# A two-layer vision tower: turning tokens for layer-1 attention with VectorE block transposes and DRAM transfers instead of TensorE transposes

## The chip, the core and the metric

The kernel runs on one core of one Trainium2 chip. Its engines are TensorE (PE in the profile; PEld is its weight load), VectorE (DVE), ScalarE (ACT), GpSimd (POOL) and SyncE (SP), which here only issues DMAs. The metric is the device time of one execution in microseconds, as the median of a few runs. All data are float32.

## The reference, cut to what matters

Thirty-two images of 256 tokens with 256 features pass a tokenizer, layer 0 (gated attention, then a feed-forward on selected tokens), and layer 1. The change is in the attention of layer 1 and, for two pairs of images, in the end of layer 0. Per image it computes:

```
x   = layernorm(h)                       # the kernel's norm; rows are tokens
k   = tanh(gelu(x @ Wk1 + bk1) @ Wk2 + bk2) * freq * pi
q   = tanh(gelu(x @ Wq1 + bq1) @ Wq2 + bq2) * freq * pi
V   = x @ Wv + bv
r_t = sum over s <= t, k-phases of cos(k_s - q_t) * V_s  / sqrt(64 (t+1))
h   = h + x + (layernorm(r) * ln_w + ln_b) @ Wo + bo
```

The products x @ Wk1 and x @ Wq1 contract over features. TensorE contracts over partitions, so it needs x with features on partitions (`dxT`), while the norm yields x with tokens on partitions (`dx`). Making `dxT` from `dx` is what is changed.

## The kernel before, in words

The whole tower stays on the chip. `H[b]` holds image b as [128 partitions, 2 chunks of 128 tokens, 256 features]. The stages run one after the other: tokenizer, attention of layer 0, feed-forward of layer 0 (`step_c`, images in groups of four), attention of layer 1 (functions with `_d`), feed-forward of layer 1. The order of every engine's instructions in these stages is written out by hand: an engine does its own in program order and waits on semaphores for the others. SP is an engine of this kind too, its DMAs stand in one queue in program order.

Layer-1 attention goes by pairs of images, 16 of them. The loop over t at line 988 starts one pair every three steps, and in each step calls the functions for whichever pairs they are due (`do(step, which)` calls `which` for pair u where t = 3u + step). For pair u these are, in the order of a pair's life:

- step 0: `norm_d` (L789), which makes the two images' `dx` from `H` on VectorE: per image two short operations for `one` (L796, L797) and two TENSOR_SCALARs of 128x256 (L799). `dx` has four buffers, one per image, so two pairs' worth.
- step 1: `turn` (L891). It calls `transposed` (L180), in which TensorE transposes 128x128 blocks, eight per pair (L189), into two PSUM banks; ScalarE (L194) and VectorE (L196) copy these to `dxT`, [128 features, 2 halves, 512 tokens]. Also `residual_d` (L805): GpSimd adds `dx` and a bias row to `H`, four additions of 128x512 (L808, L809).
- step 2: `hidden` (L895) twice, for keys and queries: matmuls on `dxT` and a Gelu.
- step 3: `phases` (L906): matmuls, tanh, then VectorE arithmetic (L923 to L927) and a sine on ScalarE.
- step 4: `match` (L930): scores of all token pairs on TensorE; VectorE multiplies them by a causal matrix into `dat` (L943).
- step 5: `memory` (L946): TensorE with `dx` as weights and `dat`; it is the last reader of the pair's `dx`.
- step 6: `output` (L959): matmuls with `wvo` into four banks, and statistics on VectorE (L967).
- step 7: `add_output` (L974) and `stats_e` (L979).

A steady round of TensorE, three steps, is so in program order: turn of pair u, match of u-1, hidden of u, memory of u-1, phases of u, output of u-1. In the step of hidden u and memory u-1 the buffers that pair u+1 will get for its `dx` are those that memory u-1 reads. Calls out of this order are made at the start: pairs 0 and 1 are normed at the end of layer 0's feed-forward (L873 to L875, into buffers `cx`), both are turned early (t = 1 and 2), and pair 1's steps are drawn ahead. At t = 6, 9 and 12 the last group of layer 0's `step_c` fetches and updates its four images (fetches on GpSimd, updates L849 and L124 on VectorE).

Within layer 0's feed-forward, buffers `cs` [128, 4, 256], two of them, receive a group's selected tokens (`first_ranks`, L220), and `made` (L823) stores its results to DRAM through SP (L830, `results`).

Of the kernel before, what the change touches and what calls it, by code (L numbers as in the profile page):

```python
# [33 lines left out]
F32 = mybir.dt.float32  # L34
# [6 lines left out]
P = 128  # L41
B, N, D = 32, 256, 256
NC = N // P
# [37 lines left out]
def vit_tower(tc, a, out):  # L81

    nc = tc.nc
# [13 lines left out]
    def bank():  # L97
        return ppool.tile([P, 512], F32, name="bank", tag="bank")
# [19 lines left out]
    def over(ap, shape, axis):  # L118
        return ap.unsqueeze(axis).to_broadcast(shape)
# [46 lines left out]
    def at(pair, b):  # L166

        st, rs = pair[b // HALF]
        return st, rs, b % HALF
# [10 lines left out]
    def transposed(xT, xs, copy):  # L180


        w = len(xs) * N
        for k in range(2):
            p = bank()
            for j, x in enumerate(xs):
                for c in range(NC):
                    o = j * N + c * P
                    nc.tensor.transpose(p[:, o : o + P], x[:, c, k * P : (k + 1) * P], ident)  # L189
            copy(k, xT[:, k, :], p[:, 0:w])  # L190
# [13 lines left out]
    pdram = passing_x.enter_context(tc.tile_pool(name="c_d", bufs=1, space=bass.MemoryType.DRAM))  # L204
# [8 lines left out]
    p0 = region_c0.enter_context(tc.tile_pool(name="c_0", bufs=1, reuse_waits="tile"))  # L213
# [59 lines left out]
    with (  # L273
# [7 lines left out]
        for k, n in enumerate(PARTS):  # L281
            f = sum(PARTS[:k])
            x, w = pw.tile([P, n, N], F32, name=f"patch0_{k}"), pw.tile([P, n, D], F32, name=f"tokW{k}")
# [4 lines left out]
        p = bank()  # L288
# [62 lines left out]
        for b in range(B):  # L351
# [12 lines left out]
            if b in (B - 6, B - 4):  # L364
                u = (b - B + 6) // 2
# [39 lines left out]
    with (  # L405
# [71 lines left out]
        def turn_weights(b0):  # L477
            p = bank()
            for j in range(2):
                w = normed_c[b0][j][1]  # L480
                for c in range(NC):
                    o = j * N + c * P
                    nc.tensor.transpose(p[:, o : o + P], w[:, c : c + 1].to_broadcast([P, P]), ident)  # L483
            return p
# [17 lines left out]
        for t in range(B // 2 + 2):  # L502
# [4 lines left out]
            if t >= 4:  # L507
                turned = turn_weights(2 * (t - 4))
# [108 lines left out]
    for i in range(2):  # L617
        s, t = slice(i * HD, (i + 1) * HD), slice((1 - i) * HD, (2 - i) * HD)
# [170 lines left out]
    def norm_d(b0, s, pool, name, bufs):  # L789
        s.xs = []  # L790
        for j in range(2):
            x = pool.tile([P, NC, D], F32, name=name, bufs=bufs)
            st, rs, i = at(st_d, b0 + j)
            q = slice(i * NC, (i + 1) * NC)
            one = spool.tile([P, NC], F32, name="d_one")
            nc.vector.scalar_tensor_tensor(one, st[:, i, :, 0], -1.0, rs[:, q], ALU.mult, ALU.mult)  # L796
            nc.vector.tensor_scalar(one, one, 1.0, None, ALU.add)  # L797
            for c in range(NC):
                nc.vector.tensor_scalar(  # L799
                    x[:, c, :], H[b0 + j][:, c, :], rs[:, i * NC + c : i * NC + c + 1], one[:, c : c + 1],  # L800
                    ALU.mult, ALU.add,
                )
            s.xs.append(x)

    def residual_d(b0, s):  # L805
        for j in range(2):
            h = H[b0 + j]
            nc.gpsimd.tensor_tensor(h, h, s.xs[j], ALU.add)  # L808
            nc.gpsimd.tensor_tensor(h, h, over(add_row, [P, NC, D], 1), ALU.add)  # L809

    with region_c:
        st_d = new_stats("d")

        def hidden_c(b0, s, half):
            if half == 0:
                s.hT = p2.tile([P, 8, 4 * P], F32, name="hT")
            for m in range(4 * half, 4 * half + 4):
                p = bank()
                for k in range(2):
                    mm(p, w1[:, k, m * P : (m + 1) * P], s.xsel[:, k, :], k == 0, k == 1)  # L820
                nc.scalar.activation(s.hT[:, m, :], p, AF.Gelu_apprx_tanh, bias=col("b1", m))

        def made(b0, s, half):  # L823
            for j in range(2 * half, 2 * half + 2):
                p = bank()
                for m in range(8):
                    mm(p[:, 0:D], s.hT[:, m, j * P : (j + 1) * P], w2[:, m, :], m == 0, m == 7)
                y = p2.tile([P, D], F32, name="cy", bufs=4)
                nc.vector.tensor_tensor(y, p[:, 0:D], row_c("b2"), ALU.add)
                nc.sync.dma_start(results[b0 + j][:], y)  # L830

        def fetch(b0, s, half):
            s.y = s.y if half else []
            for b in range(b0 + 2 * half, b0 + 2 * half + 2):
                y = px.tile([P, NC, D], F32, name="cx", bufs=8)
                for c in range(NC):
                    k = b * NC + c
                    nc.gpsimd.indirect_dma_start(
                        y[:, c, :], None, results[b][:], bass.IndirectOffsetOnAxis(rank_of[:, k : k + 1], 0)
                    )  # L840
                s.y.append(y)

        def update(b0, s, half):
            for j in range(2 * half, 2 * half + 2):
                b = b0 + j
                st, rs, i = at(st_d, b)
                for c in range(NC):
                    k = b * NC + c
                    nc.vector.scalar_tensor_tensor(  # L849
                        H[b][:, c, :], s.y[j][:, c, :], w_kept[:, k : k + 1], H[b][:, c, :], ALU.mult, ALU.add  # L850
                    )
                    stats(st, i, c, H[b][:, c, :])
            pow_rstd_of(st_d, b0 + 2 * half, 2)

        ORDER_C = ((0, hidden_c, 0), (1, hidden_c, 1), (2, made, 0), (-1, turn_c, 0), (-8, first_ranks, 0),
                   (3, made, 1), (4, fetch, 0), (5, fetch, 1), (5, update, 0), (6, update, 1))

        def step_c(t):  # L860
            for at_step, do, j in ORDER_C:
                u, r = divmod(t - at_step, 4)
                if r == 0 and 0 <= u < B // 4 and (u > 1 or do is not first_ranks):
                    do(4 * u, quads[u], j)

        END_C = 4 * (B // 4 - 1) + 4
        pairs = [Pair() for _ in range(B // 2)]
        preparing = prepare()
        for t in range(END_C):
            if t == 0:  # L870
                norms_c(B - 2)
                residuals_c(B - 2)
            if t == END_C - 2:  # L873
                for u in range(2):
                    norm_d(2 * u, pairs[u], px, "cx", 8)  # L875
            step_c(t)
            if t < 2:
                ranks(B - 4 + 2 * t, turn_weights(B - 4 + 2 * t))
            if t >= 8:
                next(preparing, None)  # L880
        passing.close()
# [5 lines left out]
    with (  # L887
        tc.tile_pool(name="d_2", bufs=2, reuse_waits="tile") as p2,
        tc.tile_pool(name="d_8", bufs=8, reuse_waits="tile") as p8,
    ):  # L890
        def turn(b0, s):  # L891
            s.xT = p2.tile([P, 2, 2 * N], F32, name="dxT")
            transposed(s.xT, s.xs, copy_split)

        def hidden(b0, s, i, ms=(0, 1)):  # L895

# [91 lines left out]
        for t in range(3 * (NP - 1) + 8):  # L988
            def do(step, which, *more):
                u, r = divmod(t - step, 3)  # L990
                if r == 0 and 0 <= u < NP:
                    which(2 * u, pairs[u], *more)

            last = t == 3 * NP + 1
            if t != 4:
                do(1, turn)
            if not last:
                do(7, add_output)
            if t != 4:
                do(4, match)  # L1000
            if last:
                output(B - 4, pairs[NP - 2], (3,))
                add_output(B - 4, pairs[NP - 2])
            do(7, stats_e)
            if t != 4:
                do(1, residual_d)
            do(2, hidden, 0)
            if t == 2:
                do(2, hidden, 1)
                turn(2, pairs[1])  # L1010
            elif t == 5:
                do(2, hidden, 1, (0,))
                match(0, pairs[0])
                do(2, hidden, 1, (1,))
            else:
                do(2, hidden, 1)
            do(5, memory)
            do(3, phases)
            if t == 5:
                residual_d(2, pairs[1])  # L1020
            if t > 3:
                do(0, norm_d, p8, "dx", 4)
            if t == 3 * NP:
                output(B - 4, pairs[NP - 2], (0, 1, 2))
            else:
                do(6, output)
            if t in (6, 9, 12):
                step_c(END_C + (t - 6) // 3)
# [5 lines left out]
    with (  # L1034
# [27 lines left out]
        def turned(b, im):  # L1062
            im.xT = p1.tile([P, 2, N], F32, name="exT")
            nc.scalar.copy(im.xT.rearrange("p k n -> p (k n)"), im.pt)
# [422 lines left out]
        p = bank()  # L1487
# [381 lines left out]
```

## Time and profile before

| | us |
|---|---|
| median of 3 runs (1919.85 to 1925.09) | 1921.87 |
| the profiled execution | 1921.73 |
| its span in the profile | 1919.9 |
| PE busy | 1876.7 (98%) |
| VectorE busy | 1255.8 (65%) |
| ScalarE busy | 814.9 (42%) |
| GpSimd busy | 757.3 (39%) |
| PE transposes of layer-1 attention (L189, `cx` of pairs 0 and 1, `dx` of the others) | 128 instructions, 0.27 each |

All places in time are microseconds from the start of the span. Layer-1 attention lies between about 929 and 1272 us. In this stage DMAs move 1 to 25 GB/s, against 306 in the kernel's first slice. A line of the timeline or of the chain has the start, the duration, then the engine, source line, and operation with its tiles; what stands in brackets at its end is the engine's idle time before it and what ended it. The chain of waits follows the end of the program back from what released what, so a stretch of it that is all PE is a stretch in which nothing but PE's own work sets the time. Matmuls of float32 are listed as two instructions each, transposes as one.

### The profile page before, as it was taken

What the parts mean: (1) busy time and instruction counts of PE and PEld (TensorE: products, weight loads), DVE (VectorE), ACT (ScalarE), POOL (GpSimd) and SP (SyncE); (2) the same over time, 40 slices, a digit from 0 to 9 for tenths busy, and PEclk for the clock granted to TensorE, in tenths of its full rate; (3) what the DMA queues carried; (4) which work ended last, traced back from release to release, by engine and by line L of the source; (5) the groups of instructions that cost most, each with busy time, mean ns of one, the idle gap of its engine ahead of it and who ended that gap; (6) DMA issues with size and microseconds to landing.
All of it is one profiled execution on the core that took longest, in us unless ns stands there. A gap on an engine that the chain in (4) does not pass through costs nothing.

```text
span 1919.9 us, 36937 instructions
## 1 busy us (share of the span) xinstructions
PE 1876.7 (98%) x14852; PEld 1337.1 (70%) x14852; DVE 1255.8 (65%) x3257; ACT 814.9 (42%) x1646; POOL 757.3 (39%) x792
## 2 busy tenths in 40 slices
PE   9999999999999999999999999999999999999993
PEld 8887666666666676766655555568878878787872
DVE  2334456565657573434366556544999999999988
ACT  0001322222222212122343444447787888878772
POOL 1224223333343344334253333334454545455453
PEclk9999999999999999999999999999999999999995
DMA  9450000000000132222000000001222222222212
GB/s 306 152 150 15 1 17 25 25 17 17 15 19 14 41 113 83 61 75 63 12 22 1 1 1 1 1 13 24 60 54 63 57 57 63 52 62 57 63 40 57
DMA packets 69506, 94.49 MB, mean 49 GB/s; under 512 B 8656, under 2 KB 51152, under 8 KB 68944
## 3 DMA queue, kind: packets, MB, share of 16 engines
q1 hardware_dynamic: 62608, 74.49, 13.6%
q0 software_dynamic: 6144, 16.79, 2.8%
q8 instruction: 119, 1.95, 0.4%
q10 hardware_dynamic: 576, 0.79, 0.1%
q14 instruction: 59, 0.48, 0.1%
HBM read 46.41 MB, written 20.97 MB: 35 GB/s over the span
## 4 chain that ended last, share of the span: by engine, by line
PE 95%; DVE 4%; issue 0%; DMA 0%; ACT 0%; POOL 0%; SPq 0%; DVEq 0%; ACTq 0%
PE bank L116 91%; PE bank L772 2%; PE bank L189 1%; DMA patch<-in_patches_dram 0%; PE bank L230 0%; PE bank L483 0%; DVE six L124 0%; DVE fout L1367 0%; DVE fout L1381 0%; DVE eo L1245 0%; DVE ranges L1268 0%; DVE six L967 0%; DVE fout L1370 0%; DVE h L849 0%; DVE ey L1330 0%
## 5 line engine op out<-in xcount | busy, mean ns | idle before, releaser
L1164 POOL TENSOR_SCALAR_AFFINE_SELECT et<-et 128x512 f32<-128x512 f32 (+1 forms) x192 | 165.7, 875 | 203.3 <-ACT et L1155 201.3
L1155 ACT ACTIVATE et<-bank 128x512 f32<-128x512 f32 x384 | 207.7, 630 | 30.6 <-PE bank L116 30.3
L116 PE MATMUL bank<-ev,et 128*64 128x68 f32 (+1 forms) x6144 | 200.6, 226 | 0.0
L116 PEld LDWEIGHTS bank<-ev,et 128*64 128x64 f32 x6144 | 193.1, 138 | 5.7 <-issue 4.7
L116 PE MATMUL bank<-g,sx 64*128 64x512 f32 (+1 forms) x512 | 177.6, 486 | 0.0
L116 PE MATMUL bank<-g,sw 64*128 64x512 f32 (+1 forms) x512 | 177.2, 486 | 0.0
L116 PE MATMUL bank<-tokW,patch 128*128 128x256 f32 x768 | 168.0, 382 | 1.7 <-DMA patch<-in_patches_dram 1.7
L116 PEld LDWEIGHTS bank<-tokW,patch 128*128 128x128 f32 x768 | 146.8, 191 | 23.2 <-issue 2.7
L116 PE MATMUL bank<-bxT,w_wuv 128*128 128x512 f32 x300 | 131.4, 592 | 0.0
L1184 ACT COPY eo<-bank 128x280 f32<-128x280 f32 x256 | 96.1, 395 | 70.1 <-PE bank L116 62.8
L116 PEld LDWEIGHTS bank<-g,sx 64*128 64x128 f32 x512 | 93.1, 187 | 31.8 <-issue 22.9
L116 PE MATMUL bank<-wvo,dm 128*128 128x512 f32 x256 | 114.3, 599 | 0.0
L116 PE MATMUL bank<-attn,bv 128*128 128x256 f32 x512 | 113.1, 379 | 0.0
L116 PE MATMUL bank<-w_wo,gT 128*128 128x256 f32 x512 | 113.1, 379 | 0.0
L116 PE MATMUL bank<-w_w,hT 128*128 128x256 f32 x512 | 113.1, 379 | 0.0
L116 PE MATMUL bank<-xsel,w_w 128*128 128x512 f32 x256 | 111.4, 592 | 0.0
L116 PEld LDWEIGHTS bank<-attn,bv 128*128 128x128 f32 x512 | 97.2, 190 | 19.6 <-issue 6.9
L124 DVE BATCH_NORM_STATS2 six<-h 128x6 f32<-128x256 f32 x256 | 105.5, 412 | 4.4
L116 PEld LDWEIGHTS bank<-w_w,hT 128*128 128x128 f32 x512 | 96.6, 190 | 15.3 <-issue 2.9
L116 PEld LDWEIGHTS bank<-g,sw 64*128 64x128 f32 x512 | 93.1, 187 | 20.1 <-issue 9.9
L116 PEld LDWEIGHTS bank<-w_wo,gT 128*128 128x128 f32 x512 | 97.2, 190 | 13.2
L116 PE MATMUL bank<-w_wuv,bxT 128*128 128x512 f32 x240 | 105.4, 592 | 0.0
(275 smaller groups left out, 3688.8 us busy)
## 6 DMA issues: line engine op xcount, KB each, us to landing
patch<-in_patches_dram SPq DMA_DIRECT2D x31, 768.0 KB, 4.8
sw<-sx SPq DMA_DIRECT2D x64, 128.0 KB, 2.4
out_dram<-fout SPq DMA_DIRECT2D x32, 256.0 KB, 2.7
both<-fxT SPq DMA_DIRECT2D x62, 128.0 KB, 2.3
both<-hx SPq DMA_DIRECT2D x62, 128.0 KB, 2.3
cs<-ranked SPq DMA_DIRECT2D x32, 128.0 KB, 3.0
results<-cy SPq DMA_DIRECT2D x32, 128.0 KB, 1.7
w_w<-in_w_dram SPq DMA_DIRECT2D x2, 1024.0 KB, 8.3
```

The source lines that it names most:

```text
L116: nc.tensor.matmul(o, lhsT, rhs, start=first, stop=last)
L124: nc.vector.bn_stats(six, x)
L189: nc.tensor.transpose(p[:, o : o + P], x[:, c, k * P : (k + 1) * P], ident)
L772: nc.tensor.transpose(p[:, o : o + P], x[:, c, k * P : (k + 1) * P], ident)
L1155: nc.scalar.activation(t2[:, i, :], p, AF.Exp)
L1164: nc.gpsimd.affine_select(out=own, in_=own, pattern=[[0, 2 * n_e], [1, P]], compare_op=ALU.is_ge, fill=0.0, base=0, channel_multiplier=-1,)
L1184: nc.scalar.copy(im.o[:, g * OC : (g + 1) * OC], p[:, 0:OC])
```

## The change

`turn`, with TensorE's transposes, is gone from this stage. In its place:

- `blocks_d`: for each image of a pair VectorE transposes 32x32 blocks of `dx` (one instruction per image, 128x512) into a buffer y; then SP issues four DMAs, one for each 32 partitions of y, that store it to a DRAM tile `d_turned`. Each stores 1024 pieces of 128 B, 512 B apart. The two image halves and the chunk order are so placed that a partition of `dxT` lies in two contiguous runs of 2 KB.
- `turned`: four DMAs on SP load `dxT`, 32 partitions each, in pieces of 2 KB (64 per DMA).
- `norm_d`, `blocks_d` and `turned` of pairs 2 to 15 are called at the end of step -1 instead of norm at the end of step 0 and turn at the start of step 1. That is behind hidden and memory of the pairs before, and ahead of the next phases on VectorE. The buffers y of these pairs are one (`dxB`).
- Pairs 0 and 1 have their blocks transposed and stored at the end of layer 0's feed-forward, right behind their norms, with the two `cs` buffers as y; they are loaded at t = 1 and t = 2 of the stage.

TensorE's remaining instructions, and those of ScalarE and GpSimd but for ScalarE's copies of `dxT`, keep their order.

```diff
+    def blocks_d(b0, s, pool, name, shape, bufs):
+        y = pool.tile(shape, F32, name=name, bufs=bufs).rearrange("p j (f t) -> p (j f t)", t=32)
+        y = y.rearrange("p (f c t) -> p f c t", f=8, t=32)
+        for j, x in enumerate(s.xs):
+            nc.vector.transpose(
+                y[:, :, j * NC : (j + 1) * NC, :].rearrange("p f c t -> p c f t"),
+                x.rearrange("p c (f t) -> p c f t", t=32),
+            )
+        s.d = pdram.tile([32, 16 * NC, 4, 32], F32, name="d_turned", bufs=2)
+        for i in range(4):
+            nc.sync.dma_start(s.d[:, :, i, :], y[32 * i : 32 * i + 32].rearrange("p f c t -> p (f c) t"))
+
...
             if t == END_C - 2:
                 for u in range(2):
                     norm_d(2 * u, pairs[u], px, "cx", 8)
+                for u in range(2):
+                    blocks_d(2 * u, pairs[u], p0, "cs", [P, 4, D], 2)
             step_c(t)
...
-        def turn(b0, s):
+        def turned(b0, s):
             s.xT = p2.tile([P, 2, 2 * N], F32, name="dxT")
-            transposed(s.xT, s.xs, copy_split)
+            d = s.d.rearrange("q (k f c) i p -> f q k (c i p)", k=2, f=4)
+            for f in range(4):
+                nc.sync.dma_start(s.xT[32 * f : 32 * f + 32], d[f])
...
-            if t != 4:
-                do(1, turn)
+            if t == 1:
+                do(1, turned)
...
             if t == 2:
                 do(2, hidden, 1)
-                turn(2, pairs[1])
+                turned(2, pairs[1])
...
             do(3, phases)
             if t == 5:
                 residual_d(2, pairs[1])
-            if t > 3:
-                do(0, norm_d, p8, "dx", 4)
+            if t > 4:
+                do(-1, norm_d, p8, "dx", 4)
+                do(-1, blocks_d, p8, "dxB", [P, 2 * NC, D], 1)
+                do(-1, turned)
```

## The prediction, made before the changed kernel was run

> **What bounds the kernel now.** I read the page's slices and chain first: PE is busy in 9 tenths or more of every slice but the last, at a granted clock of 0.99, and the chain that ended last is 95% PE. So only layer-1 attention matters, 929 to 1272 us, and there I read the chain in order of time:
>
> ```profile
> 985.86 0.59 DVE dxT L196
> 986.49 17.83 PE bank L116 x58
> ...
> 1011.38 0.59 DVE dxT L196
> 1012.01 17.84 PE bank L116 x62
> ...
> 1050.85 0.87 PE bank L189 x8
> 1051.72 20.13 PE bank L116 x80
> 1071.86 0.87 PE bank L189 x8
> ```
>
> From 1030 us on one pair takes 20.13 + 0.87 = 21.0 us, all PE; 0.87 to 0.97 of it are the eight transposes of L189. In the two pairs before, PE waited for VectorE's copy of `dxT`, which stood behind layer 0's last updates. The first matmuls on `dxT` of pairs 0, 2, 3, 4, 5 and 15 start at 929.40, 961.93, 986.49, 1012.01, 1032.16 and 1242.21. Then the timeline of one pair on PE, VectorE and GpSimd:
>
> ```profile
> 1060.13 2.78 PE L116 MATMUL bank<-dat,dx 128*128 128x256 f32 x16
> 1061.64 0.59 ACT L956 COPY dm<-bank 128x512 f32<-128x512 f32 x1 [0.62 <-PE bank L116]
> 1062.95 0.58 ACT L956 COPY dm<-bank 128x512 f32<-128x512 f32 x1 [0.72 <-PE bank L116]
> ...
> 1069.02 0.73 DVE L799 TENSOR_SCALAR dx<-h,rs_d,d_one 128x256 f32<-128x256 f32 x2
> ...
> 1071.69 1.04 PE L189 MATMUL bank<-ident,dx 128*128 128x128 f32 x8
> 1072.42 0.40 DVE L967 BATCH_NORM_STATS2 six<-bank 128x6 f32<-128x256 f32 x1
> 1074.17 3.70 PE L116 MATMUL bank<-dxT,w_wk 128*128 128x512 f32 x8
> ```
>
> Columns: start, us, engine, line. Call O the end of `output` on PE (1071.7). Then: match 1.5 us, hidden 7.0, memory 2.7, phases 1.9, output 6.9, which is 20.0 without transposes. Memory sets a pair's two `dx` free 1.5 and 2.8 us after it begins (the copies of `dm` show it). The norm today runs at 1068.6 to 1070.9, when GpSimd is idle.
>
> **Removed.** Eight transposes per pair leave PE: 0.97 us of spacing x 14 pairs, less for the first two. Their two evacuations (0.58 us ACT, 0.66 us VectorE) go too, and with the latter the wait for `dxT` in the two long pairs. Next late there would be `dat` for memory: phases' VectorE work, statistics, updates (4.2), adds (1.7) and `dat` (1.0) end 1 us before memory starts, so that wait is not replaced on VectorE. All else hidden, a pair costs 20.0 us.
>
> **Added: a round trip that must fit in one pair.** The norm of pair u moves ahead of the next phases, but its `dx` buffers (four, two pairs) are those that memory of pair u-2 reads in the same step: the norm now waits for PE. Behind it on VectorE stand the block transposes and phases' arithmetic, and SP waits for the transposes: four stores, then four loads that wait for all four stores, then hidden of pair u. The terms:
>
> Norm: 0.73 per image plus 0.3 for `d_one`. Without a collision it ends 0.7 us after the second buffer is free, hidden start + 10.5.
>
> Collision: between O+8.3 and O+13.4 GpSimd runs `residual_d`, four 128x512 additions of 1.27 us (L808, L809; now 1059.51 to 1064.70; 0.6 us earlier against O afterwards, since the statistics of L967 no longer stand behind the norm). The norm's TENSOR_SCALAR falls into this run. What that costs is in two views of layer 0, VectorE and GpSimd:
>
> ```profile
> 595.38 5.44 DVE L379 TENSOR_SCALAR cw<-cw,rows_c 128x2 f32<-128x2 f32 x1
> ```
>
> ```profile
> 595.85 2.50 POOL L256 TENSOR_TENSOR h<-h,rows_b 128x512 f32<-128x512 f32 x2
> 598.29 2.50 POOL L383 TENSOR_TENSOR h<-h,cx 128x512 f32<-128x512 f32 x2
> ```
>
> An operation of 0.23 us (its median) took 5.44: it ended when GpSimd's run of four such additions ended. I therefore let the norm begin at the end of the run, O+13.4, and end 1.9 later, O+15.3. Bounds: 0 if none collide, 1.9 at most at an unchanged pair.
>
> The Trainium skill, SBUF — State Buffer, section "Who interferes with whom", has VectorE's `tensor_scalar` and GpSimd share a port pair that whoever issues first holds for the whole instruction. By that, the norm would alternate with the additions and end near O+14.6, and the pair would be 0.3 us shorter; the row above shows a wait for four instructions, and I go by it.
>
> Block transposes: no row shows them. Two of 128x512; nearest rows 0.35 per 512 elements (L926, half of 0.69), 0.66 (the copy of L196), 1.27 (GpSimd). An added instruction can't cost less than nothing. I take 0.66 as the copy moves the same elements: 1.3 together, O+16.6, to 2.5 at worst.
>
> Stores: 4096 pieces of 128 B per pair. No store of such pieces is in the trace. The nearest are 128 loads of 128 B (11 to 13 ns each on their DMA engine, from the trace's records of packets): 256 per engine x 13 = 3.3 us; ahead of it 0.8 from issue to the first packet and 0.4 behind it, both from `results`, 1.7 us to landing. That is 4.5. From the other side: the most packets that the trace has in half a microsecond (32 B to 2 KB, DMA engines full) are 267, 534 per us, so 4096 take 7.7, together 8.9. DMAs of 64 small pieces spread over 0.3 us where their packets need 0.1; four such spreads add 1.1. I take 5.6, near the loads.
>
> The Trainium skill, DMA: Bandwidth & Descriptors, section Specifications, speaks against the stores: below 512 B the DMA engines read, modify and write. Were a piece to cost what a 512 B load costs here (27 ns), stores would take 8.1 us and a pair 23.4; no run yet shows it.
>
> Loads: four issues at 0.5 us (`cs<-ranked` goes out four in 1.85), of 128 KB in 2 KB pieces; such four last landed about 3.3 us after the first issue. 3.4 with the waits; to 4.5 if each takes the median of 3.0 below.
>
> ```profile
> cs<-ranked SPq DMA_DIRECT2D x32, 128.0 KB, 3.0
> results<-cy SPq DMA_DIRECT2D x32, 128.0 KB, 1.7
> ```
>
> **The sum per pair.** The loads land at O + 16.6 + W + 3.5, W being the stores' time and 0.1 for semaphores. PE wants them at O + 21.5 + S', S' being the stall of the pair before, since the collision is tied to O while PE has moved on by S'. So S = W - 1.4 - S'; on average S = (W - 1.4)/2 = 2.1 us, and a pair takes 22.1. (Where the stall exceeds 3.5 the run is over before memory ends, and S = W - 4.7.) Phases' arithmetic starts at O+16.6 instead of O+16.2 and its sine is ready near O+20.6, before match at O+22.1: covered; if not, match waits too.
>
> **The start.** Pair 0's loads stand on SP behind layer 0's last `results` store, whose data is ready at 928.75: issue from 929.2, landing 932.6, hidden at 932.7 instead of 929.40: +3.3. Layer 0's four block transposes (2.6 us) and eight issues (4 us) lie in VectorE and SP idle time (VectorE waits 4.9 us for PE at 917.97). Pair 1's transposes were mostly hidden behind a Gelu (0.1 saved), pair 2's save 0.97 and its round trip fits (13 us after the norm, no collision): hidden of pair 2 at 964.2. Then 13 pairs x 22.1 = 287.3: pair 15 at 1251.5 against 1242.2, **+9.3 us**. The profiled execution took 1921.73 (span 1919.9), 0.1 below the median of 1921.87, so the sum is 1931.
>
> **Rivals.** (1) *The round trip fits: faster.* Place: hidden's wait for the loads. If GpSimd's run doesn't hold the norm (S = W - 4.7) and the stores go at the loads' rate (W = 4.5), S is 0 and 13 pairs x 20.0 end at 1224.2: 18 us less, 1904. For: the 13 ns row, idle DMA (share 0.00 to 0.02 in this stage). Against: the 5.44 us row. It decides below S = 1.38, where gain and loss cancel.
> (2) *Nearly even.* The run holds the norm, the stores go at the loads' rate: S = 1.55, 13 x 21.55: +2, 1924.
> (3) *Stores are slow.* W = 8.9 gives S = 4.0 on average: 13 x 24.0, +34, 1956. For: no store of small pieces in the trace; against: 1 KB stores take 44 ns, as loads do.
> That the change does not do what it says: the instructions' order shows L189 gone from this stage and the rest as told; only its effect is open.
>
> **How the numbers follow.** About 0.3% (5.8 us) is what a measurement of this kernel can tell from no change, S from 0.94 to 1.83. Forecast (W above 5.1, held norm, up to 1940): 0.39. Slow stores: 0.20. Nearly even: 0.18. Fits: 0.23. So faster 0.23, same 0.18, slower 0.59. The range leaves out a tenth on each side: 1906 to 1957; the forecast's own is 1928 to 1940.
>
> **What would show it.** In the profile after: L189 gone from 929 on; the pair's period (22.1); PE idle before the first matmul on `dxT`, released by a DMA; L799 or L797 long where L808 and L809 run; 128x512 block transposes near 0.66; `d_turned` landing (W less the issues) and `dxT` landing; hidden of pair 0 near 932.7. A period of 20.0 with no idle PE proves rival 1. I would be wrong if the stores or the collision are far from W = 5.6 and O+15.3: 1 us of W is 0.5 us of each of 13 pairs.

## The result and the profile after

| | before | after |
|---|---|---|
| runs, median (lowest to highest) | 1922.47 us (1919.85 to 1925.09) | 1942.26 us (1940.88 to 1943.6) |
| profiled execution (its span) | 1921.73 (1919.9) | 1943.6 (1941.8) |
| TensorE busy | 1876.7 us | 1869.5 us |
| mean granted TensorE clock | 0.987 | 0.982 |
| DMA packets under 512 B | 8656 | 76240 |

The changed kernel is slower: ratio 1.0105, 95% interval 1.0089 to 1.0121, 19.8 us between the medians where +9.3 was forecast. The spans of the two profiled executions differ by 21.9 us. 2.9 of these arise before 172 us, where the two kernels are the same (the first matmuls on the patches wait 2.8 instead of 1.7 us and then take 162.09 instead of 159.09; the granted clock is 0.50 from 8.38 to 15.21 us in this execution and 1.00 in that of before), so 19.0 us are left to explain. "Net" below means less these 2.9.

TensorE is busy for 7 us less, so it waits for more than it was spared. The chain that ended last is now 90% PE instead of 95%. In order of time, one steady pair of it:

```profile
1083.08 18.66 PE bank L116 x60
1101.74 0.24 SPq L909
...
1103.30 3.02 DMA dxT<-d_turned
...
1106.41 0.67 PE bank L116
```

The columns are start, us, and what. The chain leaves TensorE at 1101.74, before its work ends, because what ends its wait for 1106.41 is the last of four loads: SP issues them from 1101.40, one every 0.63 us, and the last lands 3.02 us after its issue. From the first issue to hidden's first matmul these are 5.0 us. The timeline of the same pair, on all engines, has the whole round trip:

```profile
1083.08 5.37 PE L116 MATMUL bank<-dxT,w_wk 128*128 128x512 f32 x8 [2.32 <-DMA dxT<-d_turned]
...
1091.72 2.78 PE L116 MATMUL bank<-dat,dx 128*128 128x256 f32 x16
...
1093.23 0.74 DVE L799 TENSOR_SCALAR dx<-h,rs_d,d_one 128x256 f32<-128x256 f32 x2 [6.91 <-PE bank L116]
...
1094.54 0.74 DVE L799 TENSOR_SCALAR dx<-h,rs_d,d_one 128x256 f32<-128x256 f32 x2 [0.30 <-PE bank L116]
1095.19 1.30 DVE L809 STREAM_TRANSPOSE dxB<-dx 128x512 f32<-128x512 f32 x2
...
1096.52 2.75 SPq L815 DMA_DIRECT2D d_turned<-dxB  x4
...
1101.40 2.49 SPq L909 DMA_DIRECT2D dxT<-d_turned  x4
```

In brackets stands the idle time before, and what ended it. The norm (L799) waits 6.91 us for memory's matmuls, which free its buffer. After it come block transposes 1.30, stores 4.9 (1096.52 to 1101.40), loads 5.0, and hidden again. Hidden's own first eight matmuls took 5.37 us, not 3.67: the granted clock was halved after the wait. In the table by stretches (stretch, its length, TensorE busy and its instructions, granted clock, share of the DMA engines, GB/s):

```profile
1082.00:1083.00 1.00, 0.00 (x0) 1.00 0.16 57
...
1084.00:1085.00 1.00, 1.00 (x2) 0.50 0.00 0
...
1087.00:1088.00 1.00, 1.00 (x4) 1.00 0.00 0
```

The clock is 1.00 while TensorE stands and 0.50 when it works again. Each such window lasts 3.41 us and costs TensorE 1.7 us. And on the page, issue to landing:

```profile
dxT<-d_turned SPq DMA_DIRECT2D x64, 128.0 KB, 3.0
...
d_turned<-dxB SPq DMA_DIRECT2D x56, 128.0 KB, 2.7
```

From pair 5 on (hidden at 1037.58; its start is from here on that of its first weight load, up to 0.03 us before its first matmul) to pair 15 (1265.73) a pair takes 22.81 us on average, between 21.76 and 23.33. Worked out over the ten pairs, from one hidden to the next:

| step of the round trip | us, mean of pairs 5 to 14 |
|---|---|
| hidden's start until the first `dx` buffer is free | 8.48 |
| half clock during hidden (3 of these 10 pairs, 1.70 each) | 0.51 |
| norm, with nothing in its way | 2.05 |
| norm held by GpSimd's additions | 0.59 |
| block transposes and semaphore | 1.22 |
| first store issued to first load issued | 5.02 |
| first load issued to hidden's next start | 4.93 |
| sum | 22.80 |

### The profile page after: what moved, and what is told of

It reads as the page before. It is cut to its first block, busy times and chain, and to the rows that moved or that the text cites. A ratio compares the mean times of both kernels' runs of the same rounds, so it can differ in the third digit from the quotient of the medians.

```text
span 1941.8 us, 36931 instructions
## 1 busy us (share of the span) xinstructions
PE 1869.5 (96%) x14724; PEld 1324.6 (68%) x14724; DVE 1274.5 (66%) x3273; ACT 805.8 (41%) x1630; POOL 758.4 (39%) x792
## 2 busy tenths in 40 slices
DMA packets 141186, 111.27 MB, mean 57 GB/s; under 512 B 76240, under 2 KB 118736, under 8 KB 140624
## 4 chain that ended last, share of the span: by engine, by line
PE 90%; DVE 4%; DMA 3%; SPq 2%; issue 1%; ACT 0%; POOL 0%; DVEq 0%
PE bank L116 87%; DMA dxT<-d_turned 2%; PE bank L772 2%; SPq L909 1%; DMA d_turned<-dxB 1%; PE bank L189 1%; DVE dx L799 1%; SPq L815 0%; DMA patch<-in_patches_dram 0%; PE bank L230 0%; PE bank L483 0%; DVE dxB L809 0%; DVE fout L1385 0%; DVE fout L1399 0%; DVE eo L1263 0%
## 5 line engine op out<-in xcount | busy, mean ns | idle before, releaser
L920 ACT ACTIVATE dg<-bank,bias_d 128x512 f32<-128x512 f32 x64 | 43.8, 687 | 155.9 <-PE bank L116 155.8
L116 PEld LDWEIGHTS bank<-w_w,hT 128*128 128x128 f32 x512 | 96.6, 190 | 15.3 <-issue 2.9
L116 PEld LDWEIGHTS bank<-g,sw 64*128 64x128 f32 x512 | 93.1, 187 | 20.1 <-issue 9.9
```

Of the source, the lines that this page charges most:

```text
L116: nc.tensor.matmul(o, lhsT, rhs, start=first, stop=last)
L920: nc.scalar.activation(g[:, m, :], p, AF.Gelu, bias=bias_d[:, 2 * i + m : 2 * i + m + 1])
```

## The experiments

Theory: after the change a pair is as long as this round trip. Its longest parts are the wait for memory's buffers, the stores and the loads; collisions with GpSimd and the clock add to it. Rivals: that the norm in its new place is itself the delay; that the queue of SP is; that the clock or the collisions are most of it. All times are medians, and each ratio is against the kernel before on the same chip.

| kernel | us | ratio, 95% interval | us per pair, pairs 5 to 14 |
|---|---|---|---|
| as changed | 1942.26 | 1.0105, 1.0089 to 1.0121 | 22.81 |
| norm_only | 1919.98 | 0.999, 0.998 to 1.0 | 21.0 |
| warm | 1945.58 | 1.0125, 1.0107 to 1.0143 | 22.75 |
| warm3 | 1941.23 | 1.0092, 1.0072 to 1.0113 | 22.41 |
| no_residual | 1930.24 | 1.0038, 1.0024 to 1.0051 | 21.91 |
| split | 1946.34 | 1.0126, 1.0108 to 1.0144 | 22.97 |
| pe01 | 1938.46 | 1.009, 1.0073 to 1.0107 | 22.28 |
| six_bufs | 1912.92 | 0.9947, 0.993 to 0.9964 | 20.43 |
| six_pe01 | 1909.92 | 0.9927, 0.9911 to 0.9944 | 20.35 |
| big_stores | 1922.29 | 1.0003, 0.9993 to 1.0012 | 20.97 |
| big_late | 1937.51 | 1.0072, 1.0044 to 1.0099 | 22.30 |
| six_pe01_big | 1901.48 | 0.9891, 0.9875 to 0.9908 | 20.13 |

**norm_only: is it the moved norm?**

```diff
...
-            if t == 1:
-                do(1, turned)
+            if t != 4:
+                do(1, turn)
...
             if t > 4:
                 do(-1, norm_d, p8, "dx", 4)
-                do(-1, blocks_d, p8, "dxB", [P, 2 * NC, D], 1)
-                do(-1, turned)
```

> The norm stays one step sooner, but the tokens are turned by TensorE as before the change (no block transposes, no transfers through DRAM). Theory (the pair is set by the round trip norm, block transposes, stores, loads, hidden, and by the clock that TensorE loses while it waits for it): the sooner norm is done before output ends and nothing waits for it, so a pair takes 21.0 us as in the kernel before, and the time is 1917 to 1924. Rival (the norm in its new place, waiting for memory's buffers and held by GpSimd, is what makes a pair long): pairs stay at 22 us or more, 1934 and up.

1919.98 us, 21.0 per pair: as the kernel before. In one timeline the moved norm is held as much as anywhere, and nobody waits for it:

```profile
1105.77 2.74 DVE L799 TENSOR_SCALAR dx<-h,rs_d,d_one 128x256 f32<-128x256 f32 x2 [3.71 <-PE bank L116]
...
1115.82 1.04 PE L189 MATMUL bank<-ident,dx 128*128 128x128 f32 x8
```

The second image's norm ends at 1109.6, 6 us before TensorE turns its tokens. So the rival falls: the move alone costs nothing, and it is what stands between norm and hidden that does.

**warm and warm3: what the clock costs.**

```diff
                 p = bank()
+                for _ in range(6 if i == m == 0 and b0 > 2 else 0):
+                    mm(p[:, 0:N], zero[:, 0:P], zero)
                 for k in range(2):
```

> From the third pair on, six more matmuls of zeros (128x256, some 1.3 us together) are put ahead of hidden's first, in its own bank, where TensorE waits for the loads (1.28 to 3.16 us idle in the changed kernel's trace). Theory (4 of 10 steady pairs lose 1.7 us because the granted clock falls to 0.5 for 3.41 us after the wait, and the next norm follows memory, so the loss is lost whole): no window of 0.5 is left in the steady pairs, they fall from 22.8 to about 22.1 us, and the time from 1942 to about 1934 (1931 to 1937). Rival (the slow window only eats time that the next wait would have taken): pairs stay at 22.8, 1941 to 1944.

1945.58 us. No half-clock window is left in the steady pairs, but six such matmuls took 2.86 us (twelve instructions) and ran past the landing of the loads, so hidden waited for them; the run tells nothing of the price. (The 4 of 10 pairs in the expectation count the window at 1015.32, which lies ahead of the ten; it is 3.) Three in place of six:

> As the kernel with six matmuls of zeros, but with three (each of them is two instructions of 0.24 us on TensorE, which had been overlooked, so that the six took 2.86 us and ran past the landing of the loads in most pairs; the three take 1.4 us). Theory (the slow window after a wait costs 1.7 us in 4 of 10 steady pairs): no window of 0.5 in the steady pairs, and pairs between 21.7 and 23, by how the norm meets GpSimd's additions, 22.3 on average; the time 1935 to 1940. Rival (the slow window gives nothing away, since the norm after it no longer meets the additions): 22.7 and 1941 to 1944.

1941.23 us, a pair 22.41 instead of 22.81. Of the 0.51 us that the half clock takes in the table, taking it away gives back 0.4 a pair here, since an earlier norm meets more of GpSimd's additions. The whole time fell by 1.0 us, within the spread of the runs; of the 4.0 us that the ten steady pairs gain, pairs 2 to 4 lose 2.9, to the added matmuls and a half-clock window of 6.8 us, and 1.7 go to a window in layer 1's feed-forward that the profile of the changed kernel lacks (told at the end of the next section). The mechanism is seen in the clock; its price in the whole time stays unsettled between nothing and 4 us.

**no_residual: what GpSimd's additions cost.**

```diff
-        for j in range(2):
+        for j in range(2 if b0 < 4 else 0):
             h = H[b0 + j]
             nc.gpsimd.tensor_tensor(h, h, s.xs[j], ALU.add)
```

> The additions of the normed tokens and of the bias row to h on GpSimd are left out from the third pair on, so a part of the computation is missing. Theory (a norm instruction is held by one GpSimd addition at a time, 0.6 us a pair on average): the norm ends 2.05 us after its first buffer is free in every pair, pairs fall by 0.6 us or a little more to about 22.1, the time to 1933 to 1938. The prediction's row (the norm held until the whole run of four additions ends, 1.9 us and more a pair): pairs fall by 1.9 to about 21, 1919 to 1924.

1930.24 us, 12 less, and a pair of 21.91 (0.9 less). The norm ends 10.53 us after hidden's start in all but one of the pairs that keep the full clock, 2.05 after its buffer is free. One part is fewer clock windows (one in the steady pairs), the rest the 0.59 of the table. It lies between the two expectations. But the pair that is left over is 21.6 us with no collision and no clock window, and so still longer than the 21.0 of before: the round trip does not fit by itself.

How a norm is held, in the changed kernel (VectorE and GpSimd, 1114 to 1119 us):

```profile
1114.18 1.27 POOL L820 TENSOR_TENSOR h<-h,dx 128x512 f32<-128x512 f32 x1
1114.87 2.08 DVE L799 TENSOR_SCALAR dx<-h,rs_d,d_one 128x256 f32<-128x256 f32 x2 [4.36 <-PE bank L116]
1115.53 1.27 POOL L821 TENSOR_TENSOR h<-h,add_row 128x512 f32<-128x512 f32 x1
```

Two norm instructions of 0.41 take 2.08: the first (0.74) ends 0.15 us after the addition of 1114.18, the second (1.42) 0.15 us after the addition of 1115.53. Each is held by one addition, and then has its turn. So it is everywhere: in the eleven changed kernels that keep the additions 218 norm instructions took more than 0.45 us, none more than 1.51, and each ended 0.15 us after the end of one GpSimd instruction.

**split: is it SP's queue?**

```diff
-            nc.sync.dma_start(s.d[:, :, i, :], ...)
+            (nc.sync, nc.scalar)[i % 2].dma_start(s.d[:, :, i, :], ...)
...
-                nc.sync.dma_start(s.xT[32 * f : 32 * f + 32], d[f])
+                (nc.sync, nc.scalar)[f % 2].dma_start(s.xT[32 * f : 32 * f + 32], d[f])
...
-                do(-1, turned)
...
             do(3, phases)
+            if t > 5:
+                do(0, turned)
```

> Every second store and every second load is issued by ACT instead of SP (ACT's loads stand behind phases, so that they don't hold the sine). Theory (the four issues of 0.6 to 0.8 us one after the other on SP make up 2.8 of the 4.9 us of the stores and 2.5 of the 5.0 us of the loads): stores and loads each get shorter by 1.2 to 1.3 us, a pair by up to 2.5, to 20.3 to 21, and the time falls to 1912 to 1922. Rival (the transfers themselves and their landing set the round trip): landings get longer by what the issues save, pairs stay at 22.5 to 22.8, 1938 to 1943.

1946.34 us, 22.97 per pair. The issues did get shorter (SP's and ACT's queues in one pair):

```profile
1076.32 1.28 SPq L815 DMA_DIRECT2D d_turned<-dxB  x2
1076.33 1.57 ACTq L815 DMA_DIRECT2D d_turned<-dxB  x2
...
1081.36 1.21 SPq L909 DMA_DIRECT2D dxT<-d_turned  x2
```

The stores are issued in 1.6 instead of 2.75 us, and the first load still starts 5.04 us after the first store. The packets show why: in both kernels 4096 pieces of 128 B keep all 16 DMA engines busy for 3.0 to 3.2 us (11.8 ns each in the kernel as changed, 12.5 here). The loads gained 0.3 (4.6 us). Against that, the stores on ACT's queue delay the sine, for which match waited in nine pairs, 9.1 us in all. My theory of the issues falls for the stores: their transfers set their time.

**pe01: the start.**

```diff
-                for u in range(2):
-                    blocks_d(2 * u, pairs[u], p0, "cs", [P, 4, D], 2)
...
             if t == 1:
-                do(1, turned)
+                do(1, turn)
...
-                turned(2, pairs[1])
+                turn(2, pairs[1])
```

> Pairs 0 and 1 are turned by TensorE as before the change, the others as after it. Theory (the first hidden starts 5.0 us late because pair 0's loads stand on SP behind layer 0's last stores and then take the loads' time): the first hidden starts again 1.3 us after the last matmul of layer 0, pair 0 and 1 pay their transposes again (about 1 us of it seen), and the time falls by 4 to 5 us, to 1937 to 1939. Rival (what the start loses is caught up by waits that come after it): 1941 to 1943.

1938.46 us, 3.8 below the changed kernel; hidden of pair 0 starts at 928.39 us instead of 937.30, and 5.0 of these 8.9 us arise behind 172 us. The four runs lie between 1930.02 and 1942.93, so the size is rough; the profiled execution was the fastest, with a single clock window in this stage, and its 22.28 per pair are not typical.

**six_bufs and six_pe01: norm without the wait for memory.**

```diff
-                do(-1, norm_d, p8, "dx", 4)
+                do(-1, norm_d, p8, "dx", 6)
```

> dx has six buffers in place of four, so that the norm no longer waits for the memory matmuls of two pairs earlier. Theory (the round trip of 8.5 us to the norm's first free buffer, 2.05 norm, 1.2 transposes, 4.9 stores, 5.0 loads is longer than a pair only by what it waits for that buffer): the norm starts about 3 us after hidden instead of 8.5, the loads land before TensorE asks, pairs take 20.1 us, and the time is 1908 to 1918. Rival (the norm is then held by GpSimd's whole run of additions, which ends 8 to 9.5 us after hidden's start): the norm ends as late as before, pairs stay at 22 to 23, 1936 to 1943.

> Six buffers for dx, and pairs 0 and 1 turned by TensorE. Theory: the gains of both add up, about 4 to 5 us below the kernel with six buffers alone: 1904 to 1913, faster than the kernel before. Rival (six buffers gain nothing because the norm is held by GpSimd): as pairs 0 and 1 on TensorE alone, 1937 to 1939.

1912.92 us, 29.3 below the changed kernel and faster than the kernel before; with pairs 0 and 1 on TensorE 1909.92. One pair with six buffers:

```profile
1075.40 3.67 PE L116 MATMUL bank<-dxT,w_wk 128*128 128x512 f32 x8
...
1080.98 0.76 DVE L799 TENSOR_SCALAR dx<-h,rs_d,d_one 128x256 f32<-128x256 f32 x2
...
1082.06 2.76 DVE L799 TENSOR_SCALAR dx<-h,rs_d,d_one 128x256 f32<-128x256 f32 x2
...
1090.93 2.49 SPq L909 DMA_DIRECT2D dxT<-d_turned  x4
...
1095.91 0.67 PE L116 MATMUL bank<-dxT,w_wk 128*128 128x512 f32 x1 [0.34 <-PE bank L116]
```

The norm starts 5.6 us after hidden instead of 8.5 (later than the 3 that I expected, since VectorE has other work first) and is held by two additions. Yet the loads land almost in time, and hidden of the next pair starts 0.34 us late. From 1030 us on TensorE stood 2.5 us in all before hidden's first matmuls (1.1 of it put down to the loads), where the changed kernel had 22.6. This settles the theory's first link: with the wait for memory's buffers gone, and nothing else changed, the round trip fits but for these 2.5 us.

**big_stores, big_late and six_pe01_big: pieces and dependence.** `d_turned` gets another order in DRAM, so that the stores go in pieces of 1 KB and the loads in pieces of 128 B.

```diff
-        s.d = pdram.tile([32, 16 * NC, 4, 32], F32, ...)
+        s.d = pdram.tile([4, 4, 32, 4 * NC * 32], F32, ...)
         for i in range(4):
-            nc.sync.dma_start(s.d[:, :, i, :], y[32 * i : 32 * i + 32].rearrange("p f c t -> p (f c) t"))
+            nc.sync.dma_start(s.d[i].rearrange("f q e -> q f e"), y[32 * i : 32 * i + 32].rearrange("p f k c t -> p f (k c t)"))
...
-            for f in range(4):
-                nc.sync.dma_start(s.xT[32 * f : 32 * f + 32], d[f])
+            x = s.xT.rearrange("p k (c i t) -> p i (k c) t", i=4, t=32)
+            for i in range(4):
+                nc.sync.dma_start(x[:, i], s.d[i].rearrange("f q (e t) -> (f q) e t", t=32))
```

> The order of d_turned in DRAM is changed so that the four stores go in 512 pieces of 1 KB and the four loads in 4096 pieces of 128 B (before: stores 4096 of 128 B, loads 256 of 2 KB). Theory (the 4096 pieces keep the DMA engines busy for 3.0 of the stores' 4.9 us; the norm waits for a buffer that hidden's pair frees, so a microsecond of the stores is a microsecond of the pair): stores 3.9 to 4.1, loads as now 5.0 to 5.3, pairs shorter by 0.6 to 0.9, the time 1932 to 1938. Rival A (the prediction's slope, half of it): 1937 to 1940. Rival B (small pieces cost as much on the load side as they save on the store side, or more): 1941 and up.

1922.29 us, as the kernel before and far better than expected:

```profile
1109.15 1.77 SPq L815 DMA_DIRECT2D d_turned<-dxB  x4
1111.12 2.97 SPq L909 DMA_DIRECT2D dxT<-d_turned  x4
```

The first load is issued 2.0 us after the first store, before the last store has landed. In this order a load reads only what the store of its own number wrote; in the kernel as changed each load reads from all four. To part the two, the same kernel with the loads in the order 3, 2, 1, 0:

> As the kernel with 1 KB stores, but the four loads are issued in the opposite order, the one that needs the last store first. In the kernel with 1 KB stores a load needs only the store with its own number, which the kernel as changed does not have (there each load reads from all four stores), so two things were altered at once. Theory (most of the gain comes from loads that start before the last store has landed): stores to first load 3.9 to 4.1 us again in place of 2.0, pairs 22 to 22.6, the time 1932 to 1939. Rival (the piece size is what gained): first load 2.0 to 2.5 us after the first store, pairs 21 to 21.4, 1921 to 1926.

1937.51 us. The first load now waits for the last store: 3.6 us after the first store, against 2.0 and 5.0. So of the 20.0 us that the new order gains, 15.2 come from loads that need one store each (big_stores to big_late) and 4.8 from the pieces (big_late to the kernel as changed). Its stores are 1.4 us shorter but its loads of 128 B 0.5 longer (5.45), and a pair 0.5 shorter. The split is rough: the four runs of big_late lie between 1929.88 and 1940.27, and in its profiled execution three steady pairs had a half-clock window, some 5 us of the 15.2, where big_stores had none.

> The fastest so far (six dx buffers, pairs 0 and 1 on TensorE) with the 1 KB stores. Theory (its steady pairs wait 0 to 0.6 us for the loads where the norm met two GpSimd additions): stores 0.9 us shorter cover it, all steady pairs take 20.13, and the time falls by 1 to 3 us to 1907 to 1909. Rival (nothing waits long enough there): as before, 1909 to 1911.

1901.48 us: from pair 5 on every pair takes 20.13, no wait of TensorE is left from 1030 us on and no half-clock window in the stage. It is the fastest here, 20.1 us below the kernel before on the same chip. It is 8.4 below six_pe01, where 1 to 3 were expected; of the 5.4 us between the two profiled executions, 4.0 lie in pairs 3 and 4, which the expectation left out.

## Why the prediction was right and wrong

**Right.** What bounds a pair: hidden's wait for `dxT`, which takes the place of the transposes. L189 is gone from 929 us on. The 128x512 block transpose costs 0.66 to 0.71 us (0.66 forecast). A pair without a wait costs 20.13 (20.0), as six_pe01_big shows; phases stayed covered. The sign, and the rivals' fall: "the round trip fits" is wrong even without the additions (21.6 per pair), and slow stores did not come (W 5.0, not 8.9).

**Wrong: the loads.** "3.4 with the waits" was the term that failed: 4.93 us in the steady pairs and 5.2 for pair 0 (932.11 to 937.30). The issues are 0.63 us apart, not 0.5, so the fourth goes out 1.9 us after the first, and it still needs its 3.0. The prediction's own rows, three spaces of 0.5 and a landing of 3.0, gave 4.5; it named that as an end and took a smaller figure. Its reading that four such loads last landed about 3.3 us after the first issue does not hold for the row that it names: six times in the trace of before, four `cs<-ranked` (pieces of 1 KB) go out together, and the last lands 4.0 to 6.0 us after the first issue. This one term accounts for 1.7 us of the start (+5.0 net, 3.3 forecast). In the pair, the forecast's formula with the loads as measured (1.53 longer) and W at 5.02 gives S = (5.02 - 1.4 + 1.53) / 2 = 2.6 and 22.6 us, where 22.81 was measured. By this formula the loads add 0.77 us to each of 13 pairs, 9.9 in all, and the stores, 0.6 shorter than the forecast's 5.6, take 0.29 of each off again, 3.8 in all. (By the forecast's own figures, 0.3 us against 0.1, four spreads add 0.8 to the stores and not 1.1.)

**Wrong: why the norm is late.** The forecast let the norm begin when GpSimd's whole run ends, by the row of 5.44 us. In all 218 collisions a norm instruction is held by one addition and then goes (1.42 us where it takes 0.41). What sets the norm's start is memory's second half of the round: 8.48 us after hidden for the first buffer. By chance the two sums agree: forecast O + 15.3 is 11.7 us after hidden's start, measured 11.63. The Trainium skill, SBUF — State Buffer, section "Who interferes with whom", has the port pair held by whoever issues first for that one instruction; the traces here agree with it (218 of 218 norm instructions), and the prediction set it aside for a row that did not bear on the norm. In the thirteen traces 9 of 416 instructions like that row's, all in layer 0, took 5.4 us. Each began while GpSimd's indirect DMA (`ranked<-cx`) ran and ended with the last of the four additions behind it; but 163 others began so too and were not held, so the cause stays open.

**Left out: the clock.** The prediction priced TensorE's waits at their length only. The trace of before already had a window of half clock after a wait of 2.43 us that ended at 986.49 (the table by stretches):

```profile
985.00:986.00 1.00, 0.00 (x0) 1.00 0.43 123
986.00:987.00 1.00, 0.51 (x1) 0.92 0.46 102
987.00:988.00 1.00, 1.00 (x2) 0.50 0.35 115
```

In the changed kernel this befell pairs 0 and 4 and 3 of the 10 steady pairs, for these 0.51 us a pair in the profiled execution, of which warm3 got back 0.4.

**The slope.** "1 us of W is 0.5 us of each pair" came out near: big_late's transfers are 0.9 us shorter and its pair 0.5; in big_stores it is 2.5 and 1.84. The reason is the one given, that a shorter pair brings the norm back into the additions (it ends 12.3 us after hidden in big_stores, 11.6 as changed).

**Where the 9.7 us went** that lie between +9.3 and +19.0: 2.4 by pair 2 (1.7 of it the loads of the start; pair 0's hidden also ran at half clock until 940.22), 8.9 in the 13 pairs after it (22.79 each instead of 22.1), and 1.6 less behind pair 15's hidden, where the two kernels are alike. These 1.6 are the clock again. In both kernels TensorE waits 2.07 us in layer 1's feed-forward (for `er`, ending at 1839.03 before and at 1862.55 after). Before, the clock is 0.50 from 1840.16 to 1843.57 behind it, 1.7 us lost; after, it stays at 1.00. In the thirteen profiles the part behind pair 15's hidden takes 677.4 to 677.8 us in the ten that have such a window there and 676.1 in the three that have none. What decides is told in the last section: TensorE was busy for 1.34 us of the grid's window with that wait before, and the wait fell into two windows with 2.08 and 2.67 after.

## What to carry to other kernels

A transfer that replaces on-chip work costs its issues one after the other and then the landing of the last: take both from rows, and let each load need as few stores as possible, which here was worth roughly three times what the piece size was. Work that is moved ahead gains nothing if its output buffer comes free at the old time; count the buffers before the microseconds, one more pair of them turned +20 into -10 us here. And where a change makes TensorE wait for more than 2 us, look in the trace of before for what the granted clock does after such a wait.

## What the runs showed of the hardware

The half clock comes in windows of 3.413 us on a fixed grid: those of the changed kernel from 1000 us on start at 1015.32, 1083.58, 1196.22 and 1244.01 us, apart by 20.0, 33.0 and 14.0 times 3.413. TensorE's busy time in the grid's window before each (third column), and in two windows that no half clock followed:

```profile
1011.91:1015.32 3.41, 0.87 (x2) 1.00 0.28 94
1056.27:1059.69 3.42, 1.51 (x17) 1.00 0.47 150
1080.17:1083.58 3.41, 1.09 (x11) 1.00 0.37 118
...
1127.95:1131.37 3.42, 1.74 (x4) 1.00 0.15 46
...
1192.81:1196.22 3.41, 1.39 (x17) 1.00 0.40 138
...
1240.60:1244.01 3.41, 1.41 (x4) 1.00 0.20 70
```

Busy for 0.87 to 1.41 us (25 to 41%) the clock halved, for 1.51 and 1.74 (44% and more) it did not. In layer-1 attention of all thirteen traces the windows at full clock part the same way: at most 1.44 us busy where the next was at half clock, at least 1.47 where it was not. So a wait of 2.02 us (1196.12) cost 1.7 us more and one of 3.05 (1129.63) nothing, by where the grid lay. The Trainium skill, TensorE: Matmul & The Clock Gate, section "What's actually happening", has the same window of 3413 ns, free-running, and half clock after an idle one; here none of these four windows before was wholly idle, and a share of about 0.4 was little enough.

Stores of 128 B took 11.8 ns a piece on a DMA engine, and loads of 128 B 12.9: no sign of the read and modify ahead of small writes that the Trainium skill, DMA: Bandwidth & Descriptors, section Specifications, states and the prediction weighed. Block transposes did not wait for GpSimd: one ran in 0.70 us from 1003.19, beside an addition from 1003.20 to 1004.46.
